# A two-layer graph attention kernel: layer 0's scaling in two halves with the carried row and the table rows between them, spreading behind the one-hots, and index work in fours

## The chip, the cores and the metric

The kernel runs on one core of one Trainium2 chip. The metric is the device time of one execution in microseconds (us), lower is better. Of the kernel before there are three timed runs and one profiled execution. The engines are named as the profile names them: PE (TensorE matmul) and PEld (its weight loads), DVE (VectorE), ACT (ScalarE), POOL (GpSimd), SP (SyncE; SPq is its queue of transfers).

## The reference

A node table `x` (6250 x 256) and 200,000 edges, sorted by destination, go through a layer norm with a relu and two layers of graph attention (4 heads, then 1). Of each layer this is what is computed:

```python
te = relu(edge_attr @ We + be) * exp(x @ Wo + bo)[src][:, None]
# each node also gets a loop edge with the mean of its incoming te
hx = (x @ Wg).reshape(n, h, f)
he = (ea @ Wge).reshape(-1, h, f)
al = leaky_relu(einsum('nhf,hf->nh', hx, a_s)[src]
                + einsum('nhf,hf->nh', hx, a_d)[dst]
                + einsum('ehf,hf->eh', he, a_e), 0.2)
m  = segment_max(al, dst)
al = exp(al - m[dst])
al = al / segment_sum(al, dst)[dst]
out = segment_sum(hx[src] * al[:, :, None], dst) + b
# layer 0: x = relu(out + x); layer 1: out + x, then the two residuals
```

So for every edge a row of 256 numbers is fetched by its source, scaled by an attention weight, and added up over the edges of one destination, with a maximum over the same edges before.

## The kernel before

**Tiling.** The edges are cut into 66 *supersteps* per layer; nearly all hold 3072 edges, 24 *chunks* (`C = 24`) of 128. Since edges are sorted by destination, one superstep touches at most 112 nodes. Per superstep:

- `gather` (L1070, POOL) fetches the 24 chunks' rows from the node table in DRAM, `T`, into a tile `G` of 128 partitions x 24 x 270, one indirect DMA for each chunk. There are three such tiles, so a gather into one can only begin when the sums that read it three supersteps ago are done.
- `rphase1`, `rphase2` (L1170, L1171, L1179; PE and ACT) and `adst` (L1326, PE) make the edges' part of the logit and the destination's part, in a PSUM tile `zad`. `adst` multiplies with one-hot rows that `spread` makes (L1194, L1195; DVE): it turns the row `lb` of local destinations, loaded by SP (`load_lb`, L1095), into one-hots in place, for two supersteps (a pair, an even one and the odd one behind it) at once, and makes `Q`, with which `parts` (L1304 to L1312) selects the destinations' terms. A second call for the same pair returns at once (`if "Q" in st`).
- `edge_rows` (L1340, L1343), `logits` (L1354 to L1371), all DVE, transpose `zad` and make the logits with running maxima; `ends` (L1378, PE) and `links` (L1388, L1390 on DVE, L1395 on PE) carry the maxima across partitions; `maxima` (L1405 to L1429) ends with the weights.
- `scale` (L1460, DVE) multiplies the whole `G` by the weights, 6144 numbers per partition. `carried` (L1445 to L1450 in layer 0, DVE) adds the part of a destination that the superstep before left unfinished, into the first row of chunk 0.
- `sums` (L1472, PE): 24 products of a one-hot matrix `S` (made by `onehots`, L1288 and L1291, DVE, 3072 numbers per partition) with a chunk of `G`, added up in a PSUM tile `u`. The profile shows each as two PE records, so 48 for a superstep. `evict` (L1477, ACT) copies `u` out to `U`.
- `finish` (L1488 to L1549 and, in layer 0, L1637 and L1639 of `node_x`; DVE with three ACT instructions) ends the superstep's nodes. In layer 0 `rows1` and `rows2` (L1562, L567 on PE) make the node's row of layer 1's table, and `rows3` stores it: the addition L571 on DVE, an exponential L1574 on ACT, and transfers from SP (L1603, L1605, L1628, L1631).

**Order.** The work around the change is in an order written out by hand, in the loop of `Kernel.edges` (the program is emitted under a manual schedule: each engine runs its instructions in the order in which the code issues them). One pass of the loop over `k` has the superstep `st` of that number, the one after it, `nx`, and the ones behind, `pv` and `late`. It issues: loads; the gather for `nx` (POOL runs ahead with it as far as its three tiles allow); `logits`, `ends` of `st`; `spread` and `parts` of `nx`; `links`, `maxima` of `st`, with `rows2` of `late`, `blocks` of `nx` among them; the edge products of `nx`; `scale`, `carried`, `sums` of `st`; `rows3` of `late`; `onehots` of `nx`; `finish` of `pv`; `evict` of `st`; `rows1`; a piece of index work; `edge_rows` of `nx`.

**Index work.** The per-edge tables (local destination, penalties, last-of-segment flags) are made during layer 0, for a group of four supersteps at a time, by the generator `index_group`, 14 DVE instructions in 13 steps (L748 to L779). `index_on` advances it by 7 steps in a pass and ends it in the last pass before the group is needed; it is active in the passes with `k` = 0, 1 and 2 modulo 4, as long as there is something left, so in two of four.

Two calls in layer 0's first superstep already use pieces: `first_edges` scales and sums in four quarters. `ending` writes out the last three supersteps of each layer by itself.

Of the kernel before, what the change touches and what calls it, by code (L numbers as in the profile page):

```python
# [32 lines left out]
C = 24  # L33
# [48 lines left out]
class Kernel:  # L82
# [705 lines left out]
    def edges(self, ctx):  # L788
        nc = self.nc
        steps = self.steps  # L790
        if self.NS % 2:
            self.load_lb(1)
        pv = late = None
        self.ahead, self.rest = 1, None
        for k, st in enumerate(steps):
            nx = steps[k + 1] if k + 1 < len(steps) else None
            if st["s"] + 2 >= self.NS:
                continue
            for q in steps[k + 1:k + 3]:
                if q["L"] is st["L"] and "tw" not in q:  # L800
                    self.nodes(q)
            self.load_lb(k + 2)
            left = 99
            if self.ahead < len(self.groups):
                left = self.groups[self.ahead][0] - 2 - (self.ahead + 2 >= len(self.groups)) - k
            if self.rest is None and left <= 2:
                gi = self.index_load(self.ahead, self.xp)
                self.rest = self.index_group(self.ahead, self.xp, gi)
            if st["L"].l and (st["s"] == 2 or st["s"] + 3 == self.NS) and not hasattr(self, "flag_i"):
                self.flag()  # L810
                if self.early:
                    self.window()
            if st["s"] + 3 == self.NS:
                self.ending(st, *steps[k + 1:k + 3], pv, late, steps[k + 3] if k + 3 < len(steps) else None)
                pv = late = None
                continue
            if 3 <= k + 1 < 6 and nx["L"].l == 0:
                nx["own"] = steps[k - 2]["G"]
            if k:
                self.gather(nx)  # L820
                drain(self.logits(st))
                self.ends(st)
            self.spread(nx)
            self.parts(nx)
            y = self.rphase1(nx)
            next(y)
            if k:
                self.links(st)
            if late:
                self.rows2(late)  # L830
            self.load_fl(k + 1)
            self.blocks(nx)
            if k:
                drain(self.maxima(st))
            drain(y)
            self.load_ea(k + 2)
            self.rphase2(nx)
            self.adst(nx)
            if "S" not in st:
                self.onehots(st)  # L840
            if k:
                drain(self.scale(st))
                self.carried(st)
                self.sums(st)
            if late:
                self.rows3(late)
                late = None
            self.onehots(nx)
            if pv:
                drain(self.finish(pv))  # L850
            self.evict(st)
            if pv:
                self.rows1(pv)
                late = pv
            self.index_on(left)
            if k == 4 and self.early:
                self.lacking()
            if k >= 6:
                next(self.late, None)
                next(self.late, None)  # L860
            self.edge_rows(nx)
            if st["s"] + 4 == self.NS:
                drain(self.finish(st))
            pv = st

    def index_on(self, left):
        if self.rest is not None:
            for _ in range(7):
                next(self.rest, None)
            if left <= 0:  # L870
                drain(self.rest)
                self.ahead, self.rest = self.ahead + 1, None
# [882 lines left out]
def drain(g):  # L1755
    for _ in g:
        pass
# [85 lines left out]
```

## Time and profile before

| | |
|---|---|
| timed runs (3) | median 4757.65 us, 4755.40 to 4757.91 |
| profiled execution | 4757.82 us, span 4756.0 us |
| granted PE clock, mean | 0.742 |
| DVE in layer 0's scale (L1460), whole tile | 6.54 us |
| DVE in one-hots (L1291) | 3.36 us |
| POOL, one gather (L1070) | 0.95 us |

The page gives each engine's busy time over the span from the first to the last instruction, then the costliest groups of instructions: line, engine, operation, tiles, count, busy time and mean of one, and after the second bar the idle time of the engine ahead of these instructions with what ended it. "issue" means that the engine waited for nothing that the profile shows. A list of waits sums that idle time by what ended it. In a timeline each row has the start, the duration, the engine, the line and the tiles, and in brackets the idle time before it; neighbouring records of one kind are merged, with their count. In a table of windows each row is a stretch of time, with the busy time and the number of instructions of each engine, the granted clock, the share of DMA and GB/s.

Layer 0's loop runs from some 215 us to some 2400 us, layer 1's from some 2600 us to some 4675 us.

### The profile page before, as it was taken

What the parts mean: (1) busy time and instruction counts of PE and PEld (TensorE: products, weight loads), DVE (VectorE), ACT (ScalarE), POOL (GpSimd) and SP (SyncE); (2) the same over time, 40 slices, a digit from 0 to 9 for tenths busy, and PEclk for the clock granted to TensorE, in tenths of its full rate; (3) what the DMA queues carried; (4) which work ended last, traced back from release to release, by engine and by line L of the source; (5) the groups of instructions that cost most, each with busy time, mean ns of one, the idle gap of its engine ahead of it and who ended that gap; (6) DMA issues with size and microseconds to landing.
All of it is one profiled execution on the core that took longest, in us unless ns stands there. A gap on an engine that the chain in (4) does not pass through costs nothing.

```text
span 4756.0 us, 35152 instructions
## 1 busy us (share of the span) xinstructions
PE 2920.2 (61%) x10096; PEld 1845.5 (39%) x10096; DVE 2864.4 (60%) x6211; ACT 531.5 (11%) x1189; POOL 2999.8 (63%) x3216
## 2 busy tenths in 40 slices
PE   6565666666666666666665656665565666565556
PEld 5343343343433433433343333333343433333334
DVE  6466666666766666666674645555555545454556
ACT  4211111111111111111110000000000000000000
POOL 5356666666666666666645666666666666666664
PEclk8777777777777777777787776767676767767777
DMA  7244444444444444444443444444444444444442
GB/s 228 58 118 121 128 138 124 133 138 125 134 135 126 133 132 132 128 132 137 127 117 99 121 126 121 120 119 125 122 119 118 127 113 124 119 123 118 120 127 74
DMA packets 248234, 591.77 MB, mean 124 GB/s; under 512 B 65849, under 2 KB 105125, under 8 KB 247783
## 3 DMA queue, kind: packets, MB, share of 16 engines
q0 software_dynamic: 150048, 422.51, 34.3%
q1 hardware_dynamic: 97009, 164.82, 10.6%
q10 hardware_dynamic: 976, 2.12, 0.2%
q8 instruction: 81, 1.33, 0.1%
q14 instruction: 120, 0.98, 0.1%
HBM read 544.23 MB, written 45.36 MB: 124 GB/s over the span
## 4 chain that ended last, share of the span: by engine, by line
DVE 45%; another core or an unknown queue 17%; PE 15%; issue 15%; POOL 1%; ACT 1%; DMA 0%; DVEq 0%; SPq 0%; ACTq 0%; POOLq 0%
DVE G L1460 15%; PE u L1472 10%; DVE S L1291 6%; PE y L1170 2%; DVE rt L1340 2%; DVE lb L1194 2%; POOL G L1070 1%; DVE m L1410 1%; DVE cl L1388 1%; DVE cl L1390 1%; DVE fb L1405 1%; DVE al L1358 1%; DVE al L1356 1%; PE lf L1395 1%
## 5 line engine op out<-in xcount | busy, mean ns | idle before, releaser
L1070 POOL DMA_INDIRECT G<-T,src x3066 | 2923.9, 954 | 1650.3 <-issue 946.9
L1472 PE MATMUL u<-G,S 128*128 128x270 f32 (+1 forms) x6212 | 1704.2, 434 | 664.3 <-issue 478.5
L1472 PEld LDWEIGHTS u<-G,S 128*128 128x128 f32 x6212 | 1317.2, 214 | 1007.4 <-issue 508.7
L1460 DVE TENSOR_TENSOR G<-G,kps 128x6144 f32<-128x6144 f32 (+6 forms) x149 | 854.2, 5740 | 0.0
L1170 PE MATMUL y<-ea,webd 64*128 64x256 f32 (+2 forms) x1056 | 456.2, 808 | 424.8 <-issue 416.4
L1388 DVE TENSOR_TENSOR_SCAN cl<-fl,cl,lf 4x129 f32<-4x129 f32 (+1 forms) x130 | 61.1, 470 | 954.5 <-remote 637.4
L1291 DVE TENSOR_TENSOR S<-kps,loc 128x3072 f32<-128x3072 f32 (+1 forms) x135 | 438.1, 3245 | 4.6
L1179 PE MATMUL zad<-R,wea 128*64 128x384 f32 (+1 forms) x1056 | 298.3, 705 | 154.5 <-ACT R L1171 80.2
L1170 PEld LDWEIGHTS y<-ea,webd 64*128 64x128 f32 x1056 | 159.8, 282 | 539.0 <-issue 524.7
L1477 ACT ACTIVATE U<-u 128x270 f32<-128x270 f32 (+1 forms) x130 | 51.1, 393 | 2061.3 <-remote 1345.7
L1171 ACT ACTIVATE R<-y,webd 128x1024 f32<-128x1024 f32 (+3 forms) x264 | 235.4, 892 | 386.1 <-PE y L1170 162.5
L1179 PEld LDWEIGHTS zad<-R,wea 128*64 128x64 f32 x1056 | 85.8, 183 | 418.1 <-issue 242.9
L1340 DVE STREAM_TRANSPOSE rt<-zad 128x768 f32<-128x768 f32 (+1 forms) x130 | 125.9, 968 | 0.7 <-PE zad L1326 0.7
L567 PE MATMUL fin<-wg,h1T 128*128 128x260 f32 x264 | 123.1, 614 | 4.3 <-ACT h1T L1564 4.3
L1312 PE MATMUL zad<-a,Q 128*128 128x12 bf16 (+1 forms) x132 | 24.0, 182 | 155.1 <-issue 83.4
L1194 DVE TENSOR_TENSOR lb<-lb,kps 128x1536 bf16<-128x1536 bf16 (+1 forms) x68 | 112.9, 1661 | 0.0
L1378 PE MATMUL lf<-ident,fb 128*36 128x128 f32 (+1 forms) x132 | 43.8, 332 | 109.3 <-DVE fb L1371 53.7
L1395 PE MATMUL lf<-ident,cl 36*128 36x36 f32 (+1 forms) x132 | 38.8, 294 | 117.0 <-DVE cl L1390 98.6
L1395 PEld LDWEIGHTS lf<-ident,cl 36*128 36x128 f32 (+1 forms) x132 | 22.9, 173 | 205.9 <-DVE cl L1390 185.2
L1562 PE MATMUL fin<-ident,fb 128*128 128x128 f32 x132 | 43.2, 378 | 90.9 <-issue 90.1
L1502 ACT ACTIVATE mw<-mw,mg 128x2 f32<-128x2 f32 x66 | 19.7, 298 | 608.5 <-DVE mw L1498 450.0
L1326 PE MATMUL zad<-lb,aq 128*128 128x384 bf16 (+2 forms) x264 | 84.9, 414 | 0.0
(264 smaller groups left out, 2282.0 us busy)
## 6 DMA issues: line engine op xcount, KB each, us to landing
ea<-in_ea_dram SPq DMA_DIRECT2D x64, 768.0 KB
G<-T,src POOLq DMA_INDIRECT x3066
lb<-locrow SPq DMA_DIRECT2D x64, 384.0 KB
nd<-t1rows SPq DMA_DIRECT2D x66, 225.8 KB
tw<-nd SPq DMA_DIRECT2D x66, 225.8 KB
tw<-T SPq DMA_DIRECT2D x66, 117.2 KB
T<-t1rows SPq DMA_DIRECT2D x66, 113.8 KB
tw<-in_x_dram SPq DMA_DIRECT2D x66, 112.0 KB
```

The lines of the kernel that those rows point to most:

```text
L567: self.nc.tensor.matmul(ps[:, :L.MW], hT[:, k, :], self.wg[L.l][:, k, :], start=(k == 0), stop=(k == 1))
L1070: nc.gpsimd.indirect_dma_start(out=G[:, c, 0:L.TW], out_offset=None, in_=st.get("from", self.T[L.l])[0:self.N, :], in_offset=bass.Indirect ...
L1170: nc.tensor.matmul(y[:, i, :n], self.webd[l][r, :], ea[r, w], start=True, stop=True)
L1171: nc.scalar.activation(R[:, :, w], y[:, :, :n], AF.Relu, bias=self.be[l])
L1179: nc.tensor.matmul(st["zad"][i * PH:(i + 1) * PH, o], self.wea[l][0], R[:, i, w], start=True, stop=False)
L1194: V.tensor_tensor(lb[:, :, :n], lb[:, :, :n], self.k_part.unsqueeze(2).to_broadcast([P, i, n]), op=OP.is_equal)
L1291: nc.vector.tensor_tensor(st["S"][:, c0:c1, :], self.k_iota.unsqueeze(1).to_broadcast(w), self.loc[:, o + c0:o + c1].unsqueeze(2).to_broad ...
L1340: V.transpose(rv[:, :32 * c].rearrange("p (b n) -> p b n", b=2), z.rearrange("p (b n) -> p b n", b=2)[:, :, :16 * c])
L1388: V.tensor_tensor_scan(cl[:H, :], fl[:H, :], lf[:H, 0:P + 1], init, op0=OP.add, op1=OP.max)
L1395: nc.tensor.transpose(pc, cl[:n, 0:P], self.ident[0:n, 0:n])
L1460: nc.vector.tensor_tensor(v, v, pw[:, c0:c1, :].unsqueeze(3) .to_broadcast([P, c1 - c0, H, L.F]), op=OP.mult)
L1472: nc.tensor.matmul(st["u"][:, :L.W], S[:, i, :], G[:, i, 0:L.W], start=(j == 0), stop=(j == c - 1))
```

## The change

It concerns the passes of layer 0 with `k` of 1 or more, and the index work. Layer 1's passes issue what they did.

```diff
             if k:
-                drain(self.scale(st))
-                self.carried(st)
-                self.sums(st)
+                n = C if st["L"].l else C // 2
+                for i in range(0, C, n):
+                    drain(self.scale(st, cuts=(i, i + n)))
+                    if not i:
+                        self.carried(st)
+                        if late and n < C:
+                            self.rows3(late)
+                            late = None
+                    self.sums(st, (i, min(i + n, st["C"])))
             if late:
                 self.rows3(late)
                 late = None
             self.onehots(nx)
+            self.spread_ahead(st)
             if pv:
                 drain(self.finish(pv))
...
+    def spread_ahead(self, st):
+
+        q = self.steps[st["k"] + 2:st["k"] + 3]
+        if st["L"].l == 0 and st["k"] and q and q[0]["L"] is st["L"] and q[0]["s"] % 2 == 0 and q[0]["s"] + 3 < self.NS:
+            self.spread(q[0])
+
     def index_on(self, left):
         if self.rest is not None:
-            for _ in range(7):
+            for _ in range(4):
                 next(self.rest, None)
```

`scale` and `sums` work on chunks 0 to 11 first, then on 12 to 23; the carried row, which is needed in chunk 0, and `rows3` of the superstep two behind come between the two scalings. In passes with an even `k` (from 2 to 60) `spread` of the pair that begins two supersteps on follows `onehots`; before, the next pass, the odd one, issued it behind `logits`. The index work goes on 4 steps in a pass; the third pass ends what is left. New code shifts the lines behind `edges` by 13, so that L1460 becomes L1473 and L1194 becomes L1207.

On DVE, in an even pass of layer 0 from the scaling on, before (the rows are instructions in the engine's order; `G<-G,kps` is the scaling, `crow` the carried row, `t1rows<-fin` the table row, `S` the one-hots, `cnt<-U` the begin of `finish`):

```order
L1460 TENSOR_TENSOR G<-G,kps 128x24x256
L1445 TENSOR_TENSOR crow<-U,kps 1x256
L1448 TENSOR_TENSOR crow<-U,kps 1x4
L1449 TENSOR_TENSOR G<-G,crow 1x260
L1450 SCALAR_TENSOR_TENSOR G<-U,slink,G 1x5
L571 TENSOR_TENSOR t1rows<-fin,bias_898 128x260
L1288 COPY kps<-lastloc 128x1
L1291 TENSOR_TENSOR S<-kps,loc 128x3072
L1488 TENSOR_SCALAR cnt<-U 128x1
```

The same place in the changed kernel:

```order
L1473 TENSOR_TENSOR G<-G,kps 128x12x256
L1458 TENSOR_TENSOR crow<-U,kps 1x256
L1461 TENSOR_TENSOR crow<-U,kps 1x4
L1462 TENSOR_TENSOR G<-G,crow 1x260
L1463 SCALAR_TENSOR_TENSOR G<-U,slink,G 1x5
L571 TENSOR_TENSOR t1rows<-fin,bias_898 128x260
L1473 TENSOR_TENSOR G<-G,kps 128x12x256
L1301 COPY kps<-lastloc 128x1
L1304 TENSOR_TENSOR S<-kps,loc 128x3072
L1207 TENSOR_TENSOR lb<-lb,kps 128x1536
L1208 TENSOR_TENSOR Q<-kps,qsel 128x256
L1501 TENSOR_SCALAR cnt<-U 128x1
```

One scaling has become two, the second behind the table row, and the two instructions of `spread` (`lb`, `Q`) stand between the one-hots and `finish`.

On DVE, at the end of that even pass and the begin of the odd one, before, from the last index instructions (`gt`, `flpen`) over `edge_rows` (`rt`, `ade`) and `logits` to `parts` (`a`):

```order
L763 TENSOR_SCALAR flpen<-gt 128x96
L1340 STREAM_TRANSPOSE rt<-zad 128x768
L1343 TENSOR_REDUCE ade<-rt 128x96
L1354 TENSOR_TENSOR G<-rt,G 128x24x4
L1356 TENSOR_TENSOR al<-G 128x24x4
L1358 TENSOR_TENSOR al<-al,ade 128x24x4
L1360 SCALAR_TENSOR_TENSOR al<-al 128x96
L1369 SCALAR_TENSOR_TENSOR fb_195<-pen_184,al 128x96
L1371 SCALAR_TENSOR_TENSOR fb_195<-pen_184,al 128x96
L1194 TENSOR_TENSOR lb<-lb,kps 128x1536
L1195 TENSOR_TENSOR Q<-kps,qsel 128x256
L1304 CAST a_5917<-tw_203 128x8
```

The same place in the changed kernel, from the first index instruction on:

```order
L748 CAST gf<-gi 128x192
L753 TENSOR_TENSOR gt<-gf,base 128x96
L755 TENSOR_SCALAR loc<-gt 128x96
L761 TENSOR_TENSOR gt<-gf,before 128x96
L1353 STREAM_TRANSPOSE rt<-zad 128x768
L1356 TENSOR_REDUCE ade<-rt 128x96
L1367 TENSOR_TENSOR G<-rt,G 128x24x4
L1369 TENSOR_TENSOR al<-G 128x24x4
L1371 TENSOR_TENSOR al<-al,ade 128x24x4
L1373 SCALAR_TENSOR_TENSOR al<-al 128x96
L1382 SCALAR_TENSOR_TENSOR fb_195<-pen_184,al 128x96
L1384 SCALAR_TENSOR_TENSOR fb_195<-pen_184,al 128x96
```

Four index instructions stand before the transpose where there were seven, and `parts` follows the logits directly. Of the other ten of a group the next pass now has five, and the one after that five, where the next had seven and the one after none. On PE the order of the products is as it was; the first sum of chunk 12 now waits for DVE's second scaling.

## The prediction

> **What bounds the kernel now.** I read the page's busy shares first, then the costliest groups, then GpSimd's waits layer by layer, and last the timeline of two neighbouring supersteps engine by engine. The page and the groups:
>
> ```profile
> PE 2920.2 (61%) x10096; PEld 1845.5 (39%) x10096; DVE 2864.4 (60%) x6211; ACT 531.5 (11%) x1189; POOL 2999.8 (63%) x3216
> ...
> L1070 POOL DMA_INDIRECT G<-T,src x3066 | 2923.9, 954 | 1650.3 <-issue 946.9 <-PE fin L1562 220.4 <-remote 201.0
> ```
>
> No engine is full. POOL has the most work, nearly all of it gathers. Here is that group in a window over 58 supersteps of layer 0 (334 to 2383 us) with its first line in the list of waits, and in one over layer 1 (2650 to 4442 us):
>
> ```profile
> L1070 POOL DMA_INDIRECT G<-T,src x1393 | 1328.1, 953 | 722.5 <-issue 402.9 <-PE fin L1562 193.0 <-PE u L1472 114.3
> ...
> POOL G L1070 <- issue: 402.9, 1321, 0.6
> ...
> L1070 POOL DMA_INDIRECT G<-T,src x1254 | 1197.0, 955 | 600.0 <-issue 363.4 <-remote 158.8 <-PE y L1170 64.5
> ```
>
> 1393 gathers are 58 bursts of 24, and a gather with its "issue" gap takes 0.953 + 402.9/1321 = 1.26 us (1321 gaps, by the line from the list of waits), so a burst lasts 30 us. What is left of the idle time is one wait per superstep: (722.5 - 402.9)/58 = 5.51 us in layer 0, (600.0 - 363.4)/52.25 = 4.53 us in layer 1. A superstep is 30 us of gathers and this wait. POOL waits for a G buffer, which the sums (L1472) give back. The timeline of POOL in layer 0:
>
> ```profile
> 1212.21 0.95 POOL L1070 DMA_INDIRECT G<-T,src  x1 [0.30 <-issue]
> 1217.67 0.95 POOL L1070 DMA_INDIRECT G<-T,src  x1 [4.51 <-PE u L1472]
> ...
> 1255.20 0.95 POOL L1070 DMA_INDIRECT G<-T,src  x1 [7.44 <-PE u L1472]
> ...
> 1289.47 0.95 POOL L1070 DMA_INDIRECT G<-T,src  x1 [4.50 <-PE fin L1562]
> ```
>
> So there are short waits of 4.5 and long ones of 7.4. The sums behind the long and the short one:
>
> ```profile
> 1233.36 10.61 PE L1472 MATMUL u<-G,S 128*128 128x270 f32 x38 [2.91 <-DVE G L1450]
> 1245.12 0.39 PE L1472 MATMUL u<-G,S 128*128 128x270 f32 x1 [1.15 <-issue]
> 1247.91 0.61 PE L1472 MATMUL u<-G,S 128*128 128x270 f32 x1 [2.40 <-issue]
> 1250.02 0.61 PE L1472 MATMUL u<-G,S 128*128 128x270 f32 x1 [1.50 <-issue]
> 1251.42 3.50 PE L1472 MATMUL u<-G,S 128*128 128x270 f32 x7 [0.80 <-issue]
> ...
> 1266.72 12.21 PE L1472 MATMUL u<-G,S 128*128 128x270 f32 x45 [4.18 <-DVE crow L1448]
> 1279.10 0.39 PE L1472 MATMUL u<-G,S 128*128 128x270 f32 x1 [0.17 <-issue]
> 1281.90 0.61 PE L1472 MATMUL u<-G,S 128*128 128x270 f32 x1 [2.42 <-issue]
> ```
>
> Some 24 to 26 us after a burst's first gather PE falls from four sums a microsecond to one in 2 to 3 us, with nothing to wait for ("issue"), and recovers only after the burst's last gather. I call this the slow stretch. Sums that begin 11.5 us after the first gather (1266.72 - 1255.20) have 45 of 48 records behind them when it comes. Sums that begin 15.7 us after it (1233.36 - 1217.67) have 38, and do their last 7 in 3.50 us after it: that is the long wait. Layer 1 shows the floor:
>
> ```profile
> 3207.65 13.68 PE L1472 MATMUL u<-G,S 128*128 128x261 f32 x48 [1.86 <-DVE G L1442]
> ...
> 3227.04 0.94 POOL L1070 DMA_INDIRECT G<-T,src  x1 [0.30 <-issue]
> 3232.55 0.94 POOL L1070 DMA_INDIRECT G<-T,src  x1 [4.56 <-remote]
> ...
> 3232.31 0.39 ACT L1477 ACTIVATE U<-u 128x261 f32<-128x261 f32 x1 [20.16 <-remote]
> ```
>
> All 48 are issued by 3221.3, yet both who wait for them, ACT's eviction and POOL, go on at 3232.3, 4.5 us after the last gather. Ending the sums earlier than this buys nothing more.
>
> Why were the sums late? DVE runs into the slow stretch too. The superstep before the long wait:
>
> ```profile
> 1205.62 0.25 DVE L748 CAST gf<-gi 128x192 f32<-128x192 int32 x1
> 1208.70 0.26 DVE L753 TENSOR_TENSOR gt<-gf,base 128x96 f32<-128x96 f32 x1 [2.83 <-issue]
> ...
> 1214.99 0.21 DVE L763 TENSOR_SCALAR flpen<-gt 128x96 bf16<-128x96 f32 x1 [2.37 <-issue]
> 1215.12 0.98 DVE L1340 STREAM_TRANSPOSE rt<-zad 128x768 f32<-128x768 f32 x1
> ...
> 1219.28 1.73 DVE L1194 TENSOR_TENSOR lb<-lb,kps 128x1536 bf16<-128x1536 bf16 x1
> 1220.93 0.42 DVE L1195 TENSOR_TENSOR Q<-kps,qsel 128x256 bf16<-128x256 f32 x1
> ...
> 1221.96 0.47 DVE L1388 TENSOR_TENSOR_SCAN cl<-fl,cl,lf 4x129 f32<-4x129 f32 x1
> ...
> 1225.79 6.54 DVE L1460 TENSOR_TENSOR G<-G,kps 128x6144 f32<-128x6144 f32 x1
> 1232.25 0.40 DVE L1445 TENSOR_TENSOR crow<-U,kps 1x256 f32<-1x256 f32 x1
> ...
> 1233.23 0.41 DVE L571 TENSOR_TENSOR t1rows<-fin,bias 128x260 f32<-128x260 f32 x1
> 1233.74 3.36 DVE L1291 TENSOR_TENSOR S<-kps,loc 128x3072 f32<-128x3072 f32 x1
> ...
> 1289.53 0.47 DVE L1388 TENSOR_TENSOR_SCAN cl<-fl,cl,lf 4x129 f32<-4x129 f32 x1
> ```
>
> Seven index instructions take 9.50 us (1205.62 to 1215.12), 1.36 each. Then come the logits, the spreading (2.1 us) and the links at 1221.96, 4.3 us after POOL was released at 1217.67. After the short wait at 1289.47 they come at 1289.53, at once, though spreading stands before them there as well: that superstep had no index work. So up to 4.3 us are to be had at this place.
>
> **The change part by part.** *Scale in halves.* 6.54 us for 6144 elements becomes two of 3072; L1291 does as many elements in 3.36, so 2 x 3.36 = 6.72: 0.2 us more on DVE, on 62 supersteps. The first sum now waits for 3.36 us and the carried row, not for 6.54: it begins 3.2 us earlier. The second half is ready 3.36 + 0.41 us after the carried row, while the first 24 sum records take 24 x 10.61/38 = 6.7 us, so PE does not wait in the middle. The table row (0.41) moves ahead of the second half, so its activation on ACT and its transfers on SP come some 3 us earlier; their place in those two queues stays the same.
>
> *Spreading.* Two instructions, 1.73 + 0.42 = about 2.1 us, on every second superstep, leave the place between logits and links and go behind the one-hots, ahead of the node finish. The finish and everything behind it on DVE (index work, transpose, logits) start 2.1 us later, mostly ahead of the slow stretch; the links lose these 2.1 us. Net zero in DVE's work. It now needs its lb a superstep sooner. SP's and DVE's rows:
>
> ```profile
> 1251.39 0.02 SPq L1095 DMA_DIRECT2D lb<-locrow  x1
> ...
> 1267.11 3.36 DVE L1291 TENSOR_TENSOR S<-kps,loc 128x3072 f32<-128x3072 f32 x1
> ```
>
> The new place is at 1267.11 + 3.36 = 1270.5, 19 us after the issue. If lb were late, the finish, edge rows and logits would queue behind it; 19 us is long beside any transfer of this loop, so I cost it at nothing.
>
> *Index work in fours.* 14 instructions per four supersteps, now 4, 5, 5 and 0, not 7, 7, 0, 0. In the superstep above 3 x 1.36 = 4.1 us fewer lie before the logits. A third superstep gets 5 that had none: at best 5 x 0.26 us (L753's own duration), 1.3 us, at worst 5 x 1.36 = 6.8 us.
>
> *The sum.* Long-wait superstep: sums start at 15.7 - 4.1 - 3.2 = 8.4 us after the first gather, well under the 11.5 that ends in a short wait. Superstep with the new five: 11.5 - 3.2 + (1.3 to 6.8) = 9.6 to 15.1, where 11.5 costs 4.50 and 15.7 costs 7.44. I take the lower half, because its spreading has left the slow stretch. So nearly all waits become short. I take 4.6 us, a little over layer 1's 4.53: 58 x (5.51 - 4.6) = 53 us. The bounds: 4.2 for all gives 58 x 1.31 = 76 us; if a third of the supersteps keep long waits through the new five, some 10 us is left. Ahead of this window one more wait ends directly with the sums:
>
> ```profile
> 332.36 0.95 POOL L1070 DMA_INDIRECT G<-T,src  x1 [23.36 <-PE fin L1562]
> ```
>
> It gets 3.2 us shorter. Layer 1, the ending and the prologue keep their code. Profiled execution 4757.8 us (span 4756.0, 1.8 around it; the runs' median is 4757.65, the same): 4757.8 - 53 - 3 = 4702 us.
>
> **Rivals.** *The stretch follows the count, not the order.* Instructions from release to release of POOL, long then short:
>
> ```profile
> 1217.67:1255.20 37.53, 23.61 (x77) 14.92 (x77) 26.83 (x64) 4.33 (x11) 23.08 (x25) 0.73 0.41 113
> 1255.20:1289.47 34.27, 20.88 (x77) 13.33 (x75) 24.12 (x51) 4.33 (x11) 22.75 (x24) 0.80 0.52 145
> ```
>
> The long one has 13 more on DVE for 3.26 us, 0.25 each. If time went with the number alone, evening out would give nothing and 62 more instructions would cost 62 x 0.25 = 16 us: 4773. For it: all engines but POOL slow down together. Against it: a wait cannot fall under 4.5, so a short superstep takes a few more for nothing. [...]
>
> *DVE becomes the late one (slower).* Place: the even supersteps, where 2.1 us of spreading now stand before the finish. If PE's earlier sums bring the slow stretch forward by 3.2 us, the finish and 5 index instructions fall into it; at 1.36 us each they end after POOL's release, and links, scale and sums follow late. It decides once the sums start later than about 12.5 us after the first gather. Then each even superstep waits 7.44: 30 long waits where there are now about (319.6 - 58 x 4.5)/2.94 = 20: + 10 x 2.94 = 29 us, 4787. Against it: sums 3.2 us earlier absorb 3.2 us of lateness.
>
> *Half of it.* The halves help the long waits, the new five spoil others: 25 us, 4733.
>
> *POOL runs through.* If a release came before the burst's end, POOL would not wait: without waits 58 supersteps give 58 x 5.2 = 302 us, 4456; or the slow stretch never ends and every second step loses some 10 us. Layer 1's sums, done 6 us ahead of the burst's end and not signalled, speak against it.
>
> **How the numbers follow.** Forecast (4683 to 4725) 0.64; half of it 0.14; the count 0.09; DVE late 0.09; running through 0.04, either side. The time is the forecast's, 4702. Low 4682 is all waits at 4.2 (4757.8 - 76); high 4748 takes in "half of it" and the bound of 10 us. 0.2% is 9.5 us, about what a measurement of this kernel can tell from no change. Faster: 0.64 + 0.14 + 0.02 = 0.80; within: 0.08, most of the count rival's lower prices; slower: 0.12.
>
> **What would show it.** POOL's waits in layer 0: all 4.2 to 5, none of 7 (idle less "issue" near 270 us, from 319.6). Sums starting 8 to 12 us after the first gather, 48 records before or in the slow stretch. Two L1473 rows of 3.36 us, sums running under the second. No DVE idle before the spreading. It is wrong if long waits stay on any one superstep in four, if DVE's links come 3 us or more after POOL's release on even supersteps, or if POOL's waits are short and the time has not fallen.

## The result, and the profile after

The changed kernel takes 4783.83 us (median of 4 runs, 4782.94 to 4784.26) against 4756.52 us for the kernel before in the same comparison: a ratio of 1.0058, 95% interval 1.0041 to 1.0075. It is 27 us slower; the forecast was 4702 us, and even the range ended at 4748. The profiled execution took 4783.89 us against 4757.82, 26.1 us more.

First the heads of the two pages (before, then after) and after's line of busy time:

```profile
span 4756.0 us, 35152 instructions
```

```profile
span 4782.0 us, 35276 instructions
PE 2837.0 (59%) x10096; PEld 1792.0 (37%) x10096; DVE 2868.3 (60%) x6273; ACT 531.9 (11%) x1189; POOL 3002.5 (63%) x3216
```

There are 124 instructions more, not the 62 of the forecast. DVE has 62 of them (6211 before). The others show in the view of one line of the code, here L1485, the sums, of the changed kernel, and L1472, the same line before:

```profile
L1485 PEldq EVENT_SEMAPHORE  x203: 51/51/4785, 186.5 to 4766.3; - x102
```

```profile
L1472 PEldq EVENT_SEMAPHORE  x141: 51/51/4790, 184.4 to 4740.3; - x141
```

The sum of chunk 12 waits for its gather and now for DVE's second scaling too, and this wait is an instruction of its own on PE's queue: 203 - 141 = 62. (In e14 below, where PE has no second wait for the scaling, it is 141 again.)

Layer 0's gathers in the window of 58 supersteps (342 to 2410 us), and the first line of POOL's waits there:

```profile
L1083 POOL DMA_INDIRECT G<-T,src x1392 | 1329.4, 955 | 740.2 <-issue 405.4 <-PE u L1485 195.1 <-remote 97.3
...
POOL G L1083 <- issue: 405.4, 1330, 0.6
```

The waits are 740.2 - 405.4 = 334.8 us, 15.2 more than before (319.6), where some 50 fewer were forecast; gathers and their gaps take 3.8 us more. Ahead of the loop POOL's last long wait ends like this:

```profile
338.66 1.00 POOL L1083 DMA_INDIRECT G<-T,src  x1 [25.00 <-PE fin L1575]
```

That is 25.00 us, not 23.36 less 3.2, and at 338.66 us in place of 332.36. So of the 26.1 us, 6.3 come ahead of the loop and 19.0 in it. The same kernel before, profiled again on another chip (e5 below), reached this point at 340.0 us, and the other traces with the slow stretch reach it between 337 and 347 us, with the halves or without; so the 6.3 us need not be the change's.

Three neighbouring releases of POOL in the changed kernel, and the PE's sums in between:

```profile
1268.97 0.94 POOL L1083 DMA_INDIRECT G<-T,src  x1 [6.62 <-PE u L1485]
...
1303.29 0.94 POOL L1083 DMA_INDIRECT G<-T,src  x1 [4.29 <-remote]
...
1340.58 0.95 POOL L1083 DMA_INDIRECT G<-T,src  x1 [7.44 <-PE u L1485]
```

```profile
1277.26 10.53 PE L1485 MATMUL u<-G,S 128*128 128x270 f32 x45 [1.40 <-DVE crow L1461]
1288.01 0.39 PE L1485 MATMUL u<-G,S 128*128 128x270 f32 x1 [0.22 <-issue]
1290.13 0.39 PE L1485 MATMUL u<-G,S 128*128 128x270 f32 x1 [1.73 <-issue]
...
1313.34 8.37 PE L1485 MATMUL u<-G,S 128*128 128x270 f32 x36
1323.71 0.39 PE L1485 MATMUL u<-G,S 128*128 128x270 f32 x1 [2.00 <-issue]
...
1336.53 3.77 PE L1485 MATMUL u<-G,S 128*128 128x270 f32 x7 [1.48 <-issue]
```

The sums start where the forecast had them: 8.3 us (1277.26 - 1268.97) and 10.0 us (1313.34 - 1303.29) after the burst's first gather. But PE falls into the slow stretch (*the fall* from here on) at 1287.8 and 1321.7, 18.8 and 18.4 us after that gather, no longer at 24. In the first superstep 45 records are through by then, as before the change; in the second only 36, and POOL waits 7.44 us for the rest. Long and short waits now alternate: 29 of the 58 are over 6 us, where 17 were. Engine by engine from a release to the fall, before (a superstep with a short wait), then after (both of the above):

```profile
1255.20:1279.10 23.90, 18.34 (x71) 12.38 (x70) 20.04 (x40) 4.09 (x10) 18.10 (x20) 0.88 0.57 163
```

```profile
1268.97:1288.00 19.03, 15.88 (x71) 10.76 (x70) 17.72 (x31) 3.24 (x9) 14.46 (x16) 0.99 0.58 167
1303.29:1321.70 18.41, 15.98 (x61) 9.96 (x61) 17.05 (x36) 3.12 (x9) 14.14 (x15) 0.81 0.48 130
```

In the first of the two PE gets to the fall with the same 71 + 70 records as before, 5 us sooner; in the second it has 61 + 61. One superstep is little, so here is a count over the 57 full supersteps of this window in both traces: the fall comes 24.4 us after the burst's first gather before and 18.8 us after (medians), and by then 212 and 200 instructions of all engines but POOL, those of their sequencers included, have begun since that gather. That is 23% less time and 6% fewer instructions: the fall goes by the work rather than by the clock, though not by one exact number (187 to 226, and 180 to 210). In the first superstep DVE has 31 instructions behind it at the fall in place of 40, and does the rest slowly. On DVE there:

```profile
1272.89 3.35 DVE L1473 TENSOR_TENSOR G<-G,kps 128x3072 f32<-128x3072 f32 x1
...
1277.47 3.33 DVE L1473 TENSOR_TENSOR G<-G,kps 128x3072 f32<-128x3072 f32 x1
...
1284.31 1.74 DVE L1207 TENSOR_TENSOR lb<-lb,kps 128x1536 bf16<-128x1536 bf16 x1
...
1294.34 0.21 DVE L775 TENSOR_SCALAR isl<-gt 128x96 bf16<-128x96 f32 x1 [2.73 <-remote]
1295.75 0.21 DVE L777 TENSOR_SCALAR gt<-gt 128x96 f32<-128x96 f32 x1 [1.20 <-issue]
1297.15 0.25 DVE L779 TENSOR_REDUCE bad<-gt 128x1 f32<-128x96 f32 x1 [1.19 <-DVE gt L777]
```

The two scalings cost what was forecast (3.35 and 3.33 us), and nothing is waited for ahead of the spreading. The index instructions stand in the slow stretch all the same, 1.4 us each, because it comes sooner.

### The profile page after: what moved, and what is told of

Read it like the earlier page. It is cut to its first block, busy times and chain, and to the rows that moved or that the text cites. A ratio compares the mean times of both kernels' runs of the same rounds, so it can differ in the third digit from the quotient of the medians.

```text
span 4782.0 us, 35276 instructions
## 1 busy us (share of the span) xinstructions
PE 2837.0 (59%) x10096; PEld 1792.0 (37%) x10096; DVE 2868.3 (60%) x6273; ACT 531.9 (11%) x1189; POOL 3002.5 (63%) x3216
## 4 chain that ended last, share of the span: by engine, by line
DVE 34%; another core or an unknown queue 18%; issue 17%; PE 17%; POOL 11%; ACT 1%; DMA 1%; DVEq 0%; ACTq 0%
DVE G L1473 11%; POOL G L1083 11%; PE u L1485 10%; DVE S L1304 5%; PE y L1183 3%; DVE rt L1353 1%; DVE lb L1207 1%; DMA G<-T,src 1%; PE ps L567 1%; DVE m L1423 1%; PE zad L1192 1%; PE fin L567 1%; DVE cl L1401 1%; DVE cl L1403 1%
## 5 line engine op out<-in xcount | busy, mean ns | idle before, releaser
L1485 PE MATMUL u<-G,S 128*128 128x270 f32 (+1 forms) x6212 | 1654.6, 421 | 672.7 <-issue 545.3
L1485 PEld LDWEIGHTS u<-G,S 128*128 128x128 f32 x6212 | 1271.2, 207 | 1016.8 <-issue 618.2
L1473 DVE TENSOR_TENSOR G<-G,kps 128x3072 f32<-128x3072 f32 (+6 forms) x211 | 862.3, 4091 | 0.0
L1183 PE MATMUL y<-ea,webd 64*128 64x256 f32 (+2 forms) x1056 | 445.1, 784 | 416.2 <-issue 408.2
L1356 DVE TENSOR_REDUCE ade<-rt 128x96 f32<-128x288 f32 (+1 forms) x132 | 44.7, 338 | 137.7 <-remote 108.9
L1207 DVE TENSOR_TENSOR lb<-lb,kps 128x1536 bf16<-128x1536 bf16 (+1 forms) x68 | 113.4, 1667 | 0.0
L567 PE MATMUL fin<-wg,h1T 128*128 128x260 f32 x264 | 111.0, 562 | 2.3 <-ACT h1T L1577 2.3
L1391 PEld LDWEIGHTS lf<-ident,fb 128*36 128x36 f32 (+1 forms) x132 | 15.5, 117 | 249.5 <-DVE fb L1384 212.0
```

Of the source, the lines that this page charges most:

```text
L567: self.nc.tensor.matmul(ps[:, :L.MW], hT[:, k, :], self.wg[L.l][:, k, :], start=(k == 0), stop=(k == 1))
L1183: nc.tensor.matmul(y[:, i, :n], self.webd[l][r, :], ea[r, w], start=True, stop=True)
L1207: V.tensor_tensor(lb[:, :, :n], lb[:, :, :n], self.k_part.unsqueeze(2).to_broadcast([P, i, n]), op=OP.is_equal)
L1473: nc.vector.tensor_tensor(v, v, pw[:, c0:c1, :].unsqueeze(3) .to_broadcast([P, c1 - c0, H, L.F]), op=OP.mult)
L1485: nc.tensor.matmul(st["u"][:, :L.W], S[:, i, :], G[:, i, 0:L.W], start=(j == 0), stop=(j == c - 1))
```

## The experiments

Three theories went into the runs. *Order*: what counts is which DVE instructions stand in the slow stretch (the forecast's). *Count*, or number: a superstep can hold only so many instructions beside its gathers, and each one over that costs a fixed price wherever it stands. *Early*: earlier sums bring the slow stretch forward, and that is the loss.

The runs were on several chips, and the kernel before was timed beside them on each. On two chips (e1 to e4, e17 and e18) it took 4017 us; on the others 4763 to 4810. e5 to e8 and e13 to e16 were on one and the same chip at two times, with 4810 us the first time and 4763 the second. So all comparisons are ratios to the kernel before timed in the same group of runs, and differences in us between medians. From group to group they carry over only roughly: the change itself came out at 1.0058 (1.0041 to 1.0075) in the first comparison and at 1.0022 (1.0011 to 1.0034) in e6, intervals that don't overlap.

**The parts one by one (e1 to e4, e17, e18).** e1 is the change without its other two parts; e2, e3 and e4 are the kernel before with spreading, with fours, and with both:

```diff
+            self.spread_ahead(st)        # e2, e4
...
-            for _ in range(7):
+            for _ in range(4):           # e3, e4
                 next(self.rest, None)
```

> The kernel before, with layer 0's scale in halves and the carried and table rows between them, spreading and index work as before. Order theory (what counts is which DVE instructions stand in the slow stretch): the sums start 3.2 us earlier, the long waits shrink, some 4720 us. Count theory (a superstep can hold only so many instructions beside its gathers, each further one costs 0.25 us): 62 more instructions, some 4772 us. Early theory (the slow stretch comes earlier by as much as the sums do): every second superstep waits 7 us as in the changed kernel, some 4778 us.

> The kernel before, with spreading alone moved behind the one-hots of the even pass. Order theory: links in the odd passes come 2 us earlier and long waits shrink, some 4740 us, or, if the finish behind it is pushed into the slow stretch, some 4775 us. Count theory: no instruction is added, 4757 us within 4. Early theory: scale and sums start where they did, 4757 us or a little under it.

> The kernel before, with index work alone in 4, 5, 5 and 0 in place of 7, 7, 0 and 0. Order theory: 3 fewer of the 1.4 us instructions ahead of the logits, some 4740 us. Count theory: the same number, 4757 us within 5 (less only if the light supersteps had room to spare). Early theory: 4757 us or a little under it.

> The changed kernel without the halves: spreading moved and index work in fours, layer 0's scale whole. Order theory: the two gains add up, some 4725 us, and the halves would only help further. Count theory: 4757 us within 5, so that the whole loss of the changed kernel is the halves' (27 us). Early theory: 4757 us or less, the loss is the halves' too.

Measured: the kernel before 4016.83 us; halves 4016.82 (1.0002, 0.9992 to 1.0012), spreading 4019.85 (1.0010, 1.0000 to 1.0019), fours 4015.71 (0.9999, 0.9990 to 1.0009), both 4021.63 (1.0012, 1.0003 to 1.0022). The trace of e1 tells why none of them does more than 5 us, and that to the worse: the gathers between 340 and 2000 us, and PE's sums in two supersteps.

```profile
L1082 POOL DMA_INDIRECT G<-T,src x1317 | 1260.1, 957 | 401.2 <-issue 384.8 <-DVE mg L1530 6.1 <-DVE mg L1528 2.1
```

```profile
1221.21 11.11 PE L1484 MATMUL u<-G,S 128*128 128x270 f32 x48
...
1252.82 11.21 PE L1484 MATMUL u<-G,S 128*128 128x270 f32 x48 [0.19 <-DVE G L1462]
```

On this chip there is no slow stretch: all 48 records go through in 11 us, and POOL has 16 us of idle time beyond "issue" in 1317 gathers. Gathers run without a pause and cover everything; even the floor of some 4.5 us behind a burst, below which the forecast let no wait fall by much, is gone (no pause between two of layer 0's gathers in the loop is over 0.32 us). e17 and e18, meant to part spreading from fours on a chip with the slow stretch, met another chip without it and repeat e2 and e3:

> Spreading alone moved, scale whole, index work 7, 7, 0, 0, for a chip with the slow stretch. Spreading and fours together gained 26 us there (e9) with no instruction fewer. If the gain is from the order, by the trace of before: the long wait's sums start 2.1 us earlier of some 4 that are to be had, so spreading has a third to a half of it, 8 to 13 us faster. If spreading pushes the finish of the even passes into the slow stretch: no gain, and all of it is the fours'. Without the slow stretch: 3 us more, as in e2.

> Index work alone in 4, 5, 5 and 0, for a chip with the slow stretch. From the order: 3 fewer of the 1.4 us instructions ahead of the logits in the long superstep, 4.1 us of its lateness, against five in a superstep that had none: half to two thirds of the 26 us, 13 to 18 us faster. If the gain needs both, each alone stays within 5 us. Without the slow stretch: the same as before, as in e3.

4019.18 (1.0008, 0.9999 to 1.0018) and 4016.75 us (1.0000, 0.9991 to 1.0009). Which of the two gives the gain of e9 below stays open.

**The change, the halves and a dose of instructions (e5 to e8).** All four on one chip with the slow stretch. e5 is the kernel before for its trace, e6 the change as it is, e7 the halves alone (e1). e8 is the kernel before with:

```diff
             self.onehots(nx)
+            if k and not st["L"].l:
+                for _ in range(4):
+                    nc.vector.memset(self.mute, 0.0)
```

> The kernel before, unchanged, for its trace beside the others. In the runs of the single parts it took 4017 us, where it had taken 4757. If the slow stretch is a condition of the chip and not of the program, GpSimd runs through its gathers in this trace without a wait in a run of 4017 us, and waits 4.5 to 7.5 us behind each burst of 24 in a run of 4757 us; nothing between.

> The changed kernel, unchanged. If the chip slows PE, DVE, ACT and SP down during gathers (before at 4757 us): 4784 us, every second superstep waiting 7 us. If it does not (before at 4017 us): the scale, the sums and the index work are covered by gathers whose next tile is free long before, so the loops gain and lose nothing, and what is left is the 3 to 5 us that spreading and index work together showed (e4): 4017 to 4023 us.

> The halves alone once more, for the chip with the slow stretch. With it (before at 4757 us): order theory 4720 us, count theory 4772 us (62 instructions at 0.25 us), early theory 4778 us, every second superstep waiting 7 us. Without it (before at 4017 us): 4017 us as before.

> The kernel before with four DVE instructions added to every superstep of layer 0, behind the one-hots: each sets a column of 128 numbers that nothing reads, some 0.06 us. 248 instructions, 15 us of DVE in all. With the slow stretch (before at 4757 us): count theory 248 x 0.25 = 62 us more, 4819 us; order and early theories at most 0.3 us on each long wait, 4757 to 4765 us. Without it (before at 4017 us): 4017 us, covered by the gathers.

Measured beside 4810.22 us: the change 4823.24 (1.0022, 1.0011 to 1.0034), the halves alone 4824.75 (1.0024, 1.0009 to 1.0039), four more 4843.99 (1.0071, 1.0052 to 1.0091); e5's one execution took 4805.72. 248 instructions that compute nothing that is read, 15 to 20 us of DVE's time (59 ns each; by the pages 2886.0 us busy against 2866.3 in e5), cost 34 us: 0.14 each. DVE's time alone does not make 34 us, and order has no place for this. The halves alone lose 14.5 us, 0.12 for each of their 124; order had them gain. The change loses less here (13 us) than in the first comparison (27). In the traces, one of each, its loss over layer 0's 58 supersteps is nearly the same, 18.5 us here and 20.4 there (table below); of the rest, 6.3 us of the first comparison lie ahead of the loop, and here e5's one execution was 4.5 us under the median of its kernel.

**Without the halves, and with fewer instructions (e9 to e12).** e9 is e4. e10 makes the index tables for eight supersteps at a time; e11 does this in the changed kernel; e12 moves e8's dose to layer 1.

```diff
-            if g and cs[g[0]] == cs[s] and len(g) < 4:
+            if g and cs[g[0]] == cs[s] and len(g) < (8 if len(self.groups) > 1 else 4):
...
-        df = pool.tile([P, 2, 4 * C], F32, name="gf", bufs=1)
+        df = di.bitcast(F32)
...
-            if self.rest is None and left <= 2:
+            if self.rest is None and left <= 6:
...
-            for _ in range(7):
+            for _ in range(2):
                 next(self.rest, None)
```

> The changed kernel without the halves, for a chip with the slow stretch (before above 4700 us). Count theory, now with its price from e7 and e8 (0.11 to 0.22 us for an instruction in layer 0, waits of PE that stand as instructions of their own among them): no instruction added, the time of before within 6 us. Order theory: spreading out of the odd pass and fewer index instructions in one slow stretch gain 15 to 30 us. Early theory: no gain, no loss. Without the slow stretch (before near 4017 us): 3 to 5 us more, as in e4.

> The kernel before, with index work for eight supersteps in one group in place of four (the first group stays at four), two steps in a pass, the cast in place. The same tables from 98 DVE instructions and 14 transfers fewer; the longer instructions make up a part of DVE's time. Count theory: 112 x (0.11 to 0.22) = 12 to 25 us faster with the slow stretch. Order theory: 2 index instructions in every superstep, where four of them stood at 0 or 7, 10 to 20 us faster as well, but with long waits evenly gone. Early theory: nothing. Without the slow stretch: the same as before.

> The changed kernel with index work for eight supersteps in a group. Count theory: the halves' 62 scalings and 62 waits of PE against 112 fewer, so the time of before within 6 us with the slow stretch. Early theory: the sums are as early as in the changed kernel, so the loss stays at 10 to 27 us. Order theory: spreading, index work and halves all out of the way, 30 to 50 us faster than before. Without the slow stretch: 4017 to 4023 us.

> The kernel before with the four added DVE instructions of e8 in the supersteps of layer 1 in place of layer 0. If a superstep has an allowance beside its gathers (layer 1 has some 195 instructions from release to release, layer 0 some 250), layer 1 has room and the time stays within 6 us. If every instruction costs its price wherever it is: 240 x 0.14 = 34 us slower, as in e8. Without the slow stretch: the same as before.

Measured beside 4802.01 us: spreading and fours 4775.74 (0.9947, 0.9934 to 0.9960), eights 4779.60 (0.9957, 0.9944 to 0.9969), the change with eights 4803.34 (1.0009, 0.9998 to 1.0019), four more in layer 1 4802.98 (0.9995, 0.9984 to 1.0006).

e9 gains 26 us without one instruction fewer: here order is right, and count in its pure form is wrong. A superstep of it, the sums on PE and POOL's releases:

```profile
956.50 9.39 PE L1479 MATMUL u<-G,S 128*128 128x270 f32 x40 [1.02 <-DVE crow L1455]
...
976.92 2.43 PE L1479 MATMUL u<-G,S 128*128 128x270 f32 x4 [1.69 <-issue]
```

```profile
943.46 0.95 POOL L1077 DMA_INDIRECT G<-T,src  x1 [4.51 <-PE fin L1569]
...
979.63 0.95 POOL L1077 DMA_INDIRECT G<-T,src  x1 [6.10 <-PE u L1479]
```

The sums start 13.0 us after the burst's first gather, not 15.7, with 40 records before the fall and the last 4 after the burst, and the wait is 6.1 us. e10 gains 22 us, but it removes instructions and evens out the index work at once, so it doesn't part order from count. e11 has 98 instructions fewer than the change (35178 by the head of its page) with the sums as early, and is near the time of before: that speaks against early, though its interval and e6's overlap. e12 costs nothing: layer 1's supersteps, with 195 instructions of all engines but POOL in place of layer 0's 251 (before), have room for four more. The price was seen only in layer 0.

**The halves taken apart (e13 to e16).** e13 is e9 with two of e8's empty instructions in each superstep: 35276 instructions, exactly the changed kernel's, with sums that wait for the whole scale. e14 is the changed kernel with the second half scaled first and the table rows at their old place, so that the sums wait for both halves and PE for one of them only (35214 instructions). e15 is spreading with eights. e16 is the changed kernel with the table rows at their old place:

```diff
                     if not i:
                         self.carried(st)
-                        if late and n < C:
-                            self.rows3(late)
-                            late = None
```

> Spreading and fours (e9, 26 us faster than before) with two added DVE instructions in every superstep of layer 0, as in e8: 124 instructions, as many as the halves bring (62 scalings and 62 waits of PE), with the sums where they are in e9. If the halves lose by their number alone, this loses what they do: some 10 us slower than before. At e8's price, 34/248 = 0.14 us, it loses 17 of the 26 us, some 9 us faster than before; then what remains of the halves' 39 us, 22 us, is due to the sums starting earlier.

> The changed kernel with the two halves scaled in the other order, chunks 12 to 23 first, then 0 to 11, carried row and table row behind both: 62 scalings more than e9, but the first sum waits for both, so the sums start as late as with the whole scale and PE needs no wait in the middle. Number theory: 62 x 0.14 = 9 us of e9's 26 lost, 15 to 20 us faster than before. If two shorter scalings as such hurt: 10 to 15 us slower than before, as the changed kernel.

> Spreading moved (as in the change) and index work for eight supersteps in a group (e10), scale whole: the candidate to beat both kernels. e9 left 0.63 us over 4.6 us on each of 58 waits (5.23 on the mean, in its trace), e10 0.58 us. If number and order add up: 26 + 16 = some 40 us faster than before, no wait over 6 us. If the two only remove the same excess: some 26 us faster, as e9.

> The changed kernel with the table rows behind the second half, where they stood before: the third part of the change undone. Its addition, activation and transfers keep their number and come 3 us later. Within 5 us of the changed kernel (13 us slower than before) if it plays no part; 10 us or more faster than the changed kernel if the earlier transfers compete with the gathers.

Measured beside 4763.26 us: e13 4774.34 (1.0027, 1.0015 to 1.0039), e14 4752.49 (0.9979, 0.9968 to 0.9989), e15 4740.23 (0.9955, 0.9942 to 0.9968), e16 4767.86 (1.0012, 1.0004 to 1.0021).

e13 and e16 are the closest match: the same number of instructions, timed side by side, with sums that start 13.1 us after the first gather in e13 and 9.7 in e16 (medians). By early, e13 would be the faster one. It is not: 4774 against 4768 us, and in the traces layer 0's 58 supersteps take 2050.8 and 2052.4 us. Without the 7 us of DVE's time that e13's empty instructions take (124 x 59 ns) the two would be about level. A long wait of e13, where 36 records are through at the fall though the sums start 15.0 us (1170.70 - 1155.74) after the first gather; it is like those of the kernel before (38 records, 15.7 us):

```profile
1170.70 10.16 PE L1483 MATMUL u<-G,S 128*128 128x270 f32 x36 [2.65 <-DVE G L1461]
...
1189.43 3.54 PE L1483 MATMUL u<-G,S 128*128 128x270 f32 x9 [1.49 <-issue]
```

```profile
1155.74 0.95 POOL L1081 DMA_INDIRECT G<-T,src  x1 [4.19 <-PE u L1483]
...
1193.24 0.94 POOL L1081 DMA_INDIRECT G<-T,src  x1 [7.71 <-PE fin L1573]
```

With the gain of e9 in hand, 124 instructions cost 26 + 11 = 37 us without halves, and the halves cost 26 + 13 = 39 us (e6) or 26 + 5 = 31 us (e16). e14, with 62 of them, costs 26 - 11 = 15 us. That is 0.25 to 0.32 us for each. (e9 ran on another chip than e13 to e16, so these sums are of ratios on two chips, and may be off by some 14 us, as the change's two measurements are.) Within the one group e14 is 22 us faster than e13 with 62 instructions fewer, 0.35 each, and e15 34 us with 222 fewer, 0.15 each; on top of the kernel before the price was 0.12 to 0.14 us (e7, e8). So more instructions cost more, but not at one price, and why it differs was not tried. Early is right that early sums bring the fall forward: its median is 18.2 to 19.3 us after the first gather in every trace with early sums and 24.3 to 25.0 in every other with the slow stretch. That this is the loss, these runs do not bear out.

The table rows between the halves remain. e16, without them, is 5 us slower than before; the change is 13 us slower in e6, where the intervals overlap, and 27 us in the first comparison, where they don't. Waits over 7 us are 3 of 58 in e16 and 22 and 23 in the change's two traces. So the rows, which bring no instruction, may well take a part of the loss, up to 22 us; e16 and the change were never timed side by side, so this is open.

Layer 0's loop in the traces, one execution of each, from the first gather behind the start-up wait (332.36 us before, 338.66 after) to that of 58 supersteps on; an empty row parts the groups of runs:

| run | loop, us | waits over 6 us, of 58 | sums start, us after the first gather (median) | fall (median) |
|---|---|---|---|---|
| before | 2049.3 | 17 | 11.7 | 24.4 |
| the change | 2069.7 | 29 | 9.3 | 18.8 |
| | | | | |
| e5, before | 2076.5 | 18 | 11.5 | 24.6 |
| e6, the change | 2095.0 | 29 | 9.0 | 18.8 |
| e7, halves | 2106.4 | 31 | 8.3 | 18.4 |
| e8, four more | 2111.8 | 23 | 14.1 | 25.0 |
| | | | | |
| e9, spreading and fours | 2044.3 | 15 | 12.9 | 24.6 |
| e10, eights | 2034.9 | 8 | 12.1 | 24.5 |
| e11, the change with eights | 2076.0 | 21 | 8.3 | 18.2 |
| | | | | |
| e13, e9 and two more | 2050.8 | 15 | 13.1 | 24.7 |
| e14, halves, late sums | 2034.0 | 10 | 13.1 | 24.9 |
| e15, spreading and eights | 2018.0 | 6 | 12.0 | 24.3 |
| e16, no rows between | 2052.4 | 19 | 9.7 | 19.3 |

e7's execution was the slowest of its six.

e15 has 98 instructions fewer than e9 and is no faster by the ratio (0.9955 and 0.9947, two groups). That would fit a number below which nothing is left to gain, as a floor near 4.5 us a wait would have it (165.2/37 = 4.46 us on the mean for those of e15's waits that PE's `fin` ends). e9 and e15 beat both kernels, by some 0.5% against the kernel before.

## Why the prediction was wrong, point by point

*The bound* was read rightly: POOL's wait behind each burst, released by the sums, and the slow stretch that makes it long. Layer 1 kept its waits (264.7 and 263.5 us over 60 supersteps).

*The halves* are the step that failed. "sums start at 15.7 - 4.1 - 3.2 = 8.4 us after the first gather, well under the 11.5 that ends in a short wait": they did start at 8.3 us, and the wait was long in every second superstep. The rule behind the step, that a start by 11.5 us ends in a short wait, took the slow stretch as fixed 24 to 26 us after the first gather. It came at 18.4 and 18.8 us, and at 18.8 in the median, with nearly as many instructions done (200 against 212). Over the loop all 29 waits over 6 us follow sums that start 9.7 to 12.1 us after the first gather, the others sums that start at 8.0 to 9.3. What the sums gained in time, the stretch took back. And the halves were costed by DVE's time, at 0.2 us a superstep, and the table rows between them at nothing; alone on the kernel before they lost 14.5 us (e7, with the rows), on top of e9 31 (e16, without the rows) to 39.

*Spreading and index work* were right in mechanism and too large in size. The forecast gave all three parts together 53 us; these two alone give 26 (e9), and no run parts them on a chip with the slow stretch. The rival "half of it" put 25 us on all three parts; that this is e9's size is chance, since it counted the halves in as a gain. Whether the new five spoil short waits, as it said, no run shows.

*The count rival* came nearest and had too low a chance. It said 62 instructions at 0.25 us, 16 us, and that evening out gains nothing. It was 124 instructions, since it left out PE's waits; at the 0.25 us that it named, 31 us. That this is near the 27 measured is in part luck, since the price turned out anywhere from 0.12 to 0.35 us. And moving work without removing any gains 26 us (e9). The rival's reason, that all engines but POOL slow down together, the trace of before shows of PE, DVE and SP, not of ACT (last section). The 4.5 us in the reason against it is no bound: 19 of the 58 waits of before are shorter, down to 3.79 us. The rest of that reason, that a short superstep takes a few more for nothing, is what e12 shows of layer 1; in layer 0 the four more of e8 were not for nothing.

*DVE as the late one* forecast 4787 us with every second superstep waiting 7.4 us, and so it looks. Its first step, which the forecast lacked, is in the trace: the slow stretch comes forward, by 5 us where it said 3.2, the index instructions of the even superstep fall into it, and in the superstep behind it the links come late (1304.76, 1.5 us after the release at 1303.29). But it needs sums later than some 12.5 us after the first gather, where they started at 10.0, and at no more than 12.1 in the loop. Nor is the spreading, which it had as the cause, needed: the halves alone (e7) have 31 waits of 58 over 6 us.

*The sums of the forecast.* "If a third of the supersteps keep long waits through the new five, some 10 us is left" does not come out of its own 4.50 and 7.44 us: a third long is 5.48 us on the mean, against 5.51 measured, so 2 us is left; and its own count of 20 long waits in 58 is a third already. Layer 1's 4.53 us divides by 52.25 supersteps, where the list of waits has 53 and 233.8 us: 4.41.

*Startup*: the 3 us did not come.

## What to carry to other kernels

Before moving work ahead of a stall, ask whether the stall stands at a time or behind an amount of work; counting time and instructions up to it over many supersteps tells it, and here the earlier start only brought the stall forward (24.4 to 18.8 us after the first gather, 212 to 200 instructions). Count instructions with the waits that they bring on other engines, not only the busy time, where several engines slow down together, as PE, DVE and SP do here; to split an instruction can then be a cost, as here (the halves alone, 14.5 us in e7). And measure each part of a change alone: a gain of 26 us (e9) and a larger loss went into this one together. Time all parts in one group of runs, too: the same change lost 27 us in one and 13 in another.

## What the runs showed of the hardware

The same program, the kernel before, took 4017 us on two chips and 4757 to 4810 on the others. POOL's gathers are busy for 2922 us in e1 (the halves, as fast there as the kernel before) and 2924 us in before; the idle time ahead of them is 965.3 and 1650.3 us, 685 of the 740 us.

```profile
L1082 POOL DMA_INDIRECT G<-T,src x3066 | 2922.4, 953 | 965.3 <-issue 916.4
```

The slow stretch is thus not the program's alone; what in these chips or their state brings it, the traces don't name. In layer 0 it comes after some 200 instructions of all engines but POOL (medians of 212 before and 200 after). In the trace of before PE goes in it from 45 records of the sums in 12.21 us to one in 2.8 us (1279.10 to 1281.90), and DVE from 0.20 us between the starts of two short instructions (L1496 and L1498, 1271.03 and 1271.23) to 1.36 us for each index instruction. SP's transfer L1140 follows L1139 after 4.19 us (1281.17 to 1285.36), where L1605 follows L1603 after 0.57 us ahead of the stretch (1267.27 to 1267.84). POOL's gathers stay 1.25 us apart (1267.73 to 1268.98 ahead of it, 1281.52 to 1282.77 in it). Of ACT the traces don't show it: from 1244.5 to 1254 us, in the stretch, ACT has no instruction. Loading of code is not it, at least not each time: the table of DMA queues for 1258 to 1306 us of before, which holds the stretch from 1279 to 1288, has 1653 packets of q0 and 1313 of q1, and none of q8 and q14, the queues of kind "instruction" (81 and 120 packets in the whole span). The halves, and spreading with fours, moved the time by 14.5 and 26 us on the one kind of chip (e7, e9) and by 0.12% at most on the other (e1, e4); the whole change was not run there.
